# A GRU step's z seed moved behind the second half's new h, with one x unit between z and candidate

## The chip, the core and the metric

The kernel runs on one core of a Trainium2 chip. Its five engines work side by side, each through its own queue in order: TensorE (PE, with weight loads listed as PEld) multiplies matrices into PSUM, VectorE (DVE) and ScalarE (ACT) do element-wise work, GpSimd (POOL) does element-wise work on SBUF alone, and SyncE (SP) issues most of the transfers. The metric is the device time of one execution in microseconds, as a median over runs. Before the change it is 1341.13 us (three runs, 1340.63 to 1342.07).

## The reference

A gated recurrent unit over 128 time steps, with a batch of 64 rows and 512 features, whose outputs are added to the input. Every fourth step passes the state through one more layer.

```python
def step(h, inp):
    x_t, prop = inp
    comb = jnp.concatenate([x_t, h], axis=-1)
    z = jax.nn.sigmoid(comb @ Wz + bz)
    r = jax.nn.sigmoid(comb @ Wr + br)
    comb2 = jnp.concatenate([x_t, r * h], axis=-1)
    h_cand = jnp.tanh(comb2 @ Wh + bh)
    h_new = (1.0 - z) * h + z * h_cand
    h_next = jnp.where(prop, jnp.tanh(h_new @ Wp + bp), h_new)
    return (h_next, h_new)
```

`prop` holds where (t + 1) % 4 == 0, but for the last step. Everything is float32, the initial h is `cond_1024`, and the result is x plus the sequence of h_new.

## The kernel before

Each gate's matrix has an upper part that multiplies x_t and a lower part that multiplies h (or r * h). The lower products depend on the step before. The upper ones do not, and the kernel uses them to fill the time in which TensorE would wait.

**Two halves.** The batch is cut into two halves of 32 rows. The generator `half(h)` writes out the whole recurrence for one half, and a loop at the end takes the next piece from the half that is behind by a count of matmul columns, with the second half (h = 1) starting 700 columns later. The schedule is manual: the order in which instructions are written out is the order of each engine's queue. A matmul of one half uses 32 columns of the array, and each half has two such column groups of the four, so both halves can run at once.

**One step of a half.** On TensorE: gate R (four units), gate Z (four units), then `fill(places[0])` units of x, gate H for the candidate (four units, on rhT, the transposed r * h), then `fill(places[1])` units of x. In a step with `prop`, gate P follows (four units, on hT, the transposed new h) and then `fill(places[2])` units of x. A unit is two matmuls, each of which the trace shows as two records: 256 columns wide in the gates, 192 wide in the x units of the middle steps. Behind R come two sigmoids (`scratch_r`, L230), the product with h (`rh`, L807) and a transpose (`rhT`, L233). Behind Z of the second half come the four sigmoids for both halves at once, and `keep` = (z - 1) * h (L821). Behind H come two tanhs (`c`, L230), the product with z (L849, written over z in the PSUM bank), the subtraction of `keep` (`h`, L858) and the transpose (`hT`, L233). The next R, or P in a step with `prop`, needs that hT.

**Seeds.** The x part of a gate with its bias does not come through TensorE at the right time; it is prepared in an SBUF tile `cp`, and `seed(i, t, h)` (L371) has ScalarE copy it into the gate's PSUM place before the products with h are added onto it. R and H are seeded for each half (64 partitions), Z for both halves at once (128 partitions). The places: `rec_0` and `rec_1` hold R and H (or P) of one half each; `rec_z` is one bank that holds the sums of gate Z in its first half of the columns and z itself, later c, in the other. In a step with `prop` ScalarE also copies the bias of P (`bias_p`, L861) into `rec_0` and `rec_1`.

**Units of x.** The x products of eight steps are computed together, with fewer products than the plain way takes and more additions. They come as batches of 14 units in a fixed order of PSUM banks: two for bank a, two for x (where `scratch_x` and `scratch_y` take turns from batch to batch), two each for q and r, and then again two each for x, q and r. The second pair on x, and that on q, adds onto what the first left. When the second half has done the last unit of a pair, an `end` function is written out: for the first pair on x a copy of the bank to `cx` on ScalarE, for q a copy to `cq` (both L497), for r two additions on VectorE (L514, L515), and behind the second pairs another copy of q and three additions (L520, L523, L524). GpSimd joins the results of the batches into `cp` (L556, L561).

**Places.** `PLACES` gives the three numbers of x units for u = (t - 3) % 8, that is, for the steps 5 to 117; `HEAD` and `TAIL` give the first five and the last ten steps. Steps with u = 0 and u = 4 have `prop`. In the middle of the kernel the units of a group of eight steps add up to seven batches, so that each u always meets the same part of a batch: in step 67 (u = 0) a new batch begins.

The order on ScalarE in a step, where the seed of z stands: sigmoids of R, seed of R for each half, sigmoids of z, the seed of z for the next step, copies of `cx` or `cq` from x units behind Z, tanhs of the first half, seed of H or the bias of P, tanhs of the second half, again the seed of H or the bias of P, copies of `cx` or `cq`.

Of the kernel before, what the change touches and what calls it, by code (L numbers as in the profile page):

```python
# [18 lines left out]
def kernel(  # L19
# [28 lines left out]
    R, Z, H_ = range(3)  # L48
# [110 lines left out]
    def gate_ps(i, h):  # L159
        return rec[2][:, 0] if i == Z else rec[h][:, 0 if i == R else 1]  # L160
# [52 lines left out]
    def gate(i, h, lT, w):  # L213
        for k in range(K):
            products(gate_ps(i, h), h, lT[:, h, ts(k, V)], lambda c: quarters(w)[:, c, k])
            yield S * J
# [11 lines left out]
    def crossed(dst, h, i, func):  # L228
        for d in range(2):
            nc.scalar.activation(dst[ts(d, 2 * V)], gate_ps(i, h)[ts(h, 2 * V), d, :], func)  # L230

    def turn(dst, src):
        nc.vector.transpose(out=dst, in_=src)  # L233
# [44 lines left out]
    def sum_outer():  # L278
        for ka in range(S):
            nc.vector.tensor_sub(tw[3][:, ka], outer(1, 1, ka), outer(0, 1, ka))  # L280
            nc.vector.tensor_add(tw[2][:, ka], tw[3][:, ka], outer(0, 0, ka))
            nc.vector.tensor_sub(tw[4][:, ka], outer(1, 0, ka), tw[2][:, ka])
# [10 lines left out]
    def sum_inner_1(i, eng):  # L293
        eng.tensor_sub(inner(i, 0, 1), inner(i, 0, 1), inner(i, 0, 0))
# [17 lines left out]
    def sum_raw34(g):  # L312
        v = xT[g]
        sx[g, 34] = one.tile([P, 4, C, B], F32, tag="s73", name=f"s34r_{g}")
        four([sx[g, 34][:, n] for n in range(4)], v[:, 2], v[:, 3])
# [52 lines left out]
    def seed(i, t, h):  # L368
        if t < T:
            rows = slice(None) if i == Z else ts(h, 2 * V)  # L370
            nc.scalar.copy(  # L371
                gate_ps(i, h)[rows].rearrange("p d (c n) -> p d c n", c=C),
                G[t][rows, :, :, i, :].rearrange("p c d n -> p d c n"),
            )
# [224 lines left out]
    def pair_right(a, p1, x_, g=1):  # L599
# [2 lines left out]


    PLACES = (
        (0, 8, 6), (0, 8, 0), (6, 8, 0), (6, 8, 0), (0, 8, 6), (0, 8, 0), (6, 8, 0), (6, 6, 0),
    )
    HEAD = {0: (12, 12, 0), 1: (8, 6, 0), 2: (16, 12, 0), 3: (8, 6, 8), 4: (6, 8, 0)}
    TAIL = {
# [42 lines left out]
    def new_two(name, t):  # L651
        return shared(t, name, lambda: two.tile([P, S, J], F32, tag=name, name=f"{name}_{t}"))

    def new_turned(tag, name, t):
        return shared(t, name, lambda: new_T(tag, f"{name}_{t}"))

    def begin(t):
        u = (t - 3) % 8
        even = FIRST + 2 * ((t - 3) // 8)
        if t == 0:  # L660
            put(plain(2) + plain(3))
        elif t == 1:
            put(batch((1, 0), [(1, 1), (1, 2)]))
        elif t == 2:
            put(batch((1, 1), [(1, 10), (1, 11)]) + batch((1, 2), [(1, 8), (1, 9)]))
        elif t == 3:
            put(batches(FIRST))
        elif u == 7:
            put(batches(even + 2))
        if t == T - 10:  # L670
            put(
                batch((LAST, 0), [(LAST, 1), (LAST, 2)])
                + batch((LAST, 1), [(LAST, 10)])
                + plain_last()
            )

    def behind_r(t, duo, u):
        odd = FIRST + 2 * duo + 1
        if t == 1:
            for i in (5, 7):  # L680
                sum_inner(i, nc.gpsimd)
                sum_inner_1(i, nc.gpsimd)
        if t == 2:
            pair_left(0, 1, 2)
        elif t == 3:
            pair_right(0, 1, 10)
        if t == T - 7:
            pair_left(0, 1, 2, LAST)
        elif t == T - 6:
            pair_right(0, 1, 10, LAST)  # L690
        if t == 2:
            sum_inner(4, nc.gpsimd)
            sum_inner_1(4, nc.gpsimd)
        if u == 0 and duo >= 1 and odd - 2 < LAST:
            outer_u2(odd - 2)

    def join(t, duo, u, n):
        even, odd = FIRST + 2 * duo, FIRST + 2 * duo + 1
        if t == 0:
            join_x(0, 2 + n)  # L700
        elif t == 1:
            join_x(1, 2 + n)
        elif t == 2:
            join_x(2, n)
        elif t == 4:
            join_x(3, 2 * n)
            join_x(3, 2 * n + 1)
        elif duo >= 0 and u in (5, 6):
            join_x(even + 2, 2 * (u - 5) + n)
        elif duo >= 1 and u in (1, 3):  # L710
            join_x(odd, u - 1 + n)
# [78 lines left out]
    def half(h):  # L790

        for t in range(T):
            g, j = divmod(t, Q4)
            prop = j == CHUNK - 1 and t < T - 1
            last = t == T - 1
            duo, u = divmod(t - 3, 8)
            places = HEAD.get(t) or TAIL.get(t) or PLACES[u]
            if h == 0:
                begin(t)
            h_old, hT = state[t]  # L800

            yield from gate(R, h, hT, wh[R])
            if h == 1:
                behind_r(t, duo, u)
            rh, rhT = new_two("rh", t), new_turned("rhT", "rhT", t)
            crossed(r_, h, R, AF.Sigmoid)
            nc.vector.tensor_mul(rh[:, h, :], r_, h_old[:, h, :])  # L807
            turn(rhT[:, h, :], rh[:, h, :])
            if t != 3:
                seed(R, t + 1, h)  # L810
            if last:
                seed(H_, t, h)
            if h == 1:
                join(t, duo, u, 0)

            yield from gate(Z, h, hT, wh[Z])
            keep = new_two("keep", t)
            if h == 1:
                for i in range(S):
                    crossed(z[:, i, :], i, Z, AF.Sigmoid)  # L820
                nc.vector.scalar_tensor_tensor(  # L821
                    out=keep, in0=z, scalar=1.0, in1=h_old, op0=ALU.subtract, op1=ALU.mult
                )
                join(t, duo, u, 1)
                if t == 1:
                    sum_raw34(1)
                if t == 3:
                    for i in range(S):
                        seed(R, t + 1, i)
                seed(Z, t + 1, 0)  # L830
                if last:
                    nc.gpsimd.tensor_sub(xr[g][:, j], xr[g][:, j], keep)
                if t == 0:
                    sum_outer()
                    sum_inner(6, nc.gpsimd)
                    sum_inner_1(6, nc.gpsimd)
                if t == 2:
                    for n in range(2, 4):
                        join_x(2, n)
            yield from fill(places[0], h)  # L840
            if h == 1 and t == T - 7:
                reload()

            yield from gate(H_, h, rhT, wh[H_])
            h_new = new_two("h", t)
            cand = new_two("c", t)
            crossed(cand[:, h, :], h, H_, AF.Tanh)
            c = z[:, h, :]
            nc.vector.tensor_mul(c, cand[:, h, :], c)  # L849
            if last:  # L850
                o = xr[g][:, j, h, :]
                nc.vector.tensor_add(o, c, o)
                (nc.sync, nc.scalar)[h].dma_start(
                    out=out[ts(h, V), t, :].rearrange("b (q n) -> q b n", q=NQ), in_=o
                )
                return
            hT = new_turned("hT", "hT", t)
            nc.vector.tensor_sub(h_new[:, h, :], c, keep[:, h, :])  # L858
            turn(hT[:, h, :], h_new[:, h, :])
            if prop:  # L860
                nc.scalar.copy(gate_ps(P_, h)[ts(h, 2 * V)], bias_p[ts(h, 2 * V)])  # L861
            elif t < T - 2:
                seed(H_, t + 1, h)
            state[t + 1] = h_new, hT
            yield from fill(places[1], h)
            if h == 1 and t == 0:
                sum_outer_1()
                for i in (1, 2, 3):
                    sum_inner_1(i, nc.vector)
            if prop:  # L870
                yield from gate(P_, h, hT, wp)
                h_next = new_two("hprop", t)
                hT = new_turned("hT", "hpT", t)
                crossed(h_next[:, h, :], h, P_, AF.Tanh)
                turn(hT[:, h, :], h_next[:, h, :])
                if t < T - 2:
                    seed(H_, t + 1, h)
                state[t + 1] = h_next, hT
                yield from fill(places[2], h)
            if h == 1:  # L880
                behind_step(t, duo, u, h_new)
# [6 lines left out]
    while any(live):  # L888
        h = 0 if live[0] and (not live[1] or at[0] <= at[1]) else 1
# [45 lines left out]
```

## Time and profile before

| | |
|---|---|
| Median of three runs | 1341.13 us |
| The profiled execution, its own time | 1340.09 us |
| Span in the profile, first to last instruction | 1338.2 us |
| Mean granted TensorE clock | 0.992 |
| Chain that ended last: PE, ACT, DVE, DMA | 77%, 9%, 7%, 3% |
| Seed of z (`rec_z<-cp`, L371), 128 times | 0.377 us each |
| Tanh for 128 columns (`c`, L230), 512 times | 0.272 us each |
| Copies to `cx` and `cq` (L497) | 0.478 us each |

In the profile a group of instructions is named by line, engine, operation, and output<-input tile. Behind the bar stand its busy time, the mean of one in ns, and the idle time of the engine just before it with what ended it. In the timeline the columns are the start, the time, the engine, the line and the operation; "x2" are merged instructions, and the brackets hold idle time and what released it. The view of waits gives, for each waiting engine, line and releaser, the total, the number of times and the longest. The DMA engines are busy a tenth to a fifth of the time between the first tenth and the end of the span.

### The profile page before, as it was taken

The page shows a single profiled execution, that of the slowest core. Times are in us where ns is not written, and L with a number is a line of the kernel's source. Part 1 is how long each engine was busy: PE and PEld are TensorE (multiplying, and loading weights), DVE is VectorE, ACT ScalarE, POOL GpSimd, SP SyncE. Part 2 cuts the span into 40 slices and gives each one's busy share as a digit, 9 for nine tenths or more (in the row PEclk, how much of TensorE's full clock was granted, in tenths as well). Part 3 has the DMA queues.
Part 4 walks back from the last instruction along what each step waited for, and adds up shares of the span by engine and source line. Part 5 has one row for each costly group of instructions (what it writes and reads, how often), then busy time and mean ns, then how long its engine had stood idle before and what let it go on. Part 6 is the DMA issues. An engine that isn't in the chain of part 4 may idle for free.

```text
span 1338.2 us, 60949 instructions
## 1 busy us (share of the span) xinstructions
PE 1283.7 (96%) x26024; PEld 1117.0 (83%) x26024; DVE 771.2 (58%) x2163; ACT 837.1 (63%) x2688; POOL 886.3 (66%) x1030
## 2 busy tenths in 40 slices
PE   7989999999999999999999999999999999999977
PEld 3579888898988889888898988889888888988745
DVE  1645655656655656656556656656666566566534
ACT  1346666666666666666666666666666666666644
POOL 3568767677576776767777576777757777676410
PEclk8989999999999999999999999999999999999999
DMA  8401111101111111112101111111112111111040
GB/s 193 102 19 50 50 35 50 45 24 50 50 50 35 35 46 38 50 35 60 40 23 46 50 50 34 37 48 35 50 42 58 35 32 41 46 34 35 18 104 18
DMA packets 114710, 63.20 MB, mean 47 GB/s; under 512 B 13160, under 2 KB 109672, under 8 KB 114440
## 3 DMA queue, kind: packets, MB, share of 16 engines
q1 hardware_dynamic: 113412, 58.44, 17.3%
q8 instruction: 205, 3.36, 1.1%
q10 hardware_dynamic: 772, 0.72, 0.2%
q14 instruction: 65, 0.53, 0.1%
q0 software_dynamic: 256, 0.14, 0.1%
HBM read 42.47 MB, written 16.78 MB: 44 GB/s over the span
## 4 chain that ended last, share of the span: by engine, by line
PE 77%; ACT 9%; DVE 7%; DMA 3%; issue 2%; POOL 1%; SPq 1%; DVEq 0%; ACTq 0%; POOLq 0%
PE rec L204 35%; PE rec_z L204 15%; PE scratch_r L204 10%; PE scratch_q L204 9%; ACT rec_z L230 5%; PE scratch_x L204 3%; PE scratch_y L204 3%; PE scratch_a L204 3%; ACT c L230 2%; DVE keep L821 2%; ACT rec_z L371 2%; DVE hT L233 1%; DVE rec_z L849 1%; DVE h L858 1%; DMA wx<-in_L_cond_Wr_dram 1%
## 5 line engine op out<-in xcount | busy, mean ns | idle before, releaser
L204 PE MATMUL rec<-wh,rhT 128*32 128x256 f32 x4096 | 375.2, 381 | 4.6 <-ACT rec L371 4.4
L204 PE MATMUL rec<-wh,hT 128*32 128x256 f32 x3072 | 277.9, 380 | 14.7 <-DVE hT L233 14.7
L204 PE MATMUL rec_z<-wh,hT 128*32 128x256 f32 x3072 | 279.4, 379 | 0.0
L204 PEld LDWEIGHTS rec<-wh,rhT 128*32 128x32 f32 x4096 | 232.4, 110 | 35.6 <-ACT scratch_r L230 9.7
L230 ACT ACTIVATE scratch_r<-rec 64x128 f32<-64x128 f32 x512 | 128.0, 250 | 166.6 <-PE rec L204 95.6
L371 ACT COPY rec<-cp 64x256 f32<-64x256 f32 x512 | 189.9, 371 | 33.4 <-DVE cp L409 9.6
L204 PEld LDWEIGHTS rec<-wh,hT 128*32 128x32 f32 x3072 | 165.5, 110 | 48.0 <-ACT c L230 27.9
L230 ACT ACTIVATE rec_z<-rec_z 64x128 f32<-64x128 f32 x512 | 128.0, 250 | 108.1 <-PE rec_z L204 96.0
L204 PEld LDWEIGHTS rec_z<-wh,hT 128*32 128x32 f32 x3072 | 176.0, 110 | 14.4
L765 POOL TENSOR_TENSOR xr<-xr,h 128x256 f32<-128x256 f32 x127 | 93.0, 732 | 140.9 <-DVE h L858 122.8
L556 POOL TENSOR_TENSOR mb<-mb,mb 128x768 f32<-128x768 f32 x58 | 106.3, 1832 | 77.3 <-DVE mb L524 77.3
L230 ACT ACTIVATE c<-rec 64x128 f32<-64x128 f32 x512 | 139.0, 272 | 26.1 <-PE rec L204 16.8
L556 POOL TENSOR_TENSOR cp<-mb,mb 128x768 f32<-128x768 f32 x75 | 136.9, 1826 | 6.4 <-DVE mb L524 2.8
L556 POOL TENSOR_TENSOR cp<-mb 128x768 f32<-128x768 f32 x47 | 86.1, 1831 | 61.0 <-ACT rec L371 59.5
L821 DVE SCALAR_TENSOR_TENSOR keep<-rec_z,h 128x256 f32<-128x256 f32 x96 | 40.7, 424 | 144.9 <-ACT rec_z L230 144.9
L497 ACT COPY cq<-scratch_q 128x384 f32<-128x384 f32 (+1 forms) x214 | 102.0, 476 | 33.8 <-PE scratch_q L204 31.6
L204 PE MATMUL scratch_r<-wx,s12r 128*32 128x192 f32 x1056 | 120.9, 327 | 0.0
L204 PE MATMUL scratch_r<-tw,s 128*32 128x192 f32 x928 | 117.2, 326 | 0.0
L204 PE MATMUL scratch_r<-wx,s 128*32 128x192 f32 x928 | 107.3, 326 | 0.0
L514 DVE TENSOR_TENSOR cx<-scratch_r,cx 128x384 f32<-128x384 f32 (+1 forms) x107 | 59.2, 553 | 82.3 <-PE scratch_r L204 60.8
L849 DVE TENSOR_TENSOR rec_z<-c,rec_z 128x128 f32<-128x128 f32 x256 | 73.7, 288 | 54.8 <-ACT c L230 53.9
L204 PE MATMUL rec<-wp,hT 128*32 128x256 f32 x992 | 90.5, 380 | 12.1 <-DVE hT L233 12.1
(155 smaller groups left out, 3579.4 us busy)
## 6 DMA issues: line engine op xcount, KB each, us to landing
out_dram<-xr SPq DMA_DIRECT2D x249, 64.0 KB, 1.8
xr<-in_x_dram SPq DMA_DIRECT2D x248, 64.0 KB, 2.3
xs<-in_x_dram SPq DMA_DIRECT2D x240, 64.0 KB, 2.1
wx<-in_L_cond_Wz_dram SPq DMA_DIRECT2D x4, 256.0 KB, 8.2
wx<-in_L_cond_Wh_dram SPq DMA_DIRECT2D x4, 256.0 KB, 10.3
wh<-in_L_cond_Wr_dram SPq DMA_DIRECT2D x4, 256.0 KB, 9.0
wh<-in_L_cond_Wz_dram SPq DMA_DIRECT2D x4, 256.0 KB, 4.2
wh<-in_L_cond_Wh_dram SPq DMA_DIRECT2D x4, 256.0 KB, 7.4
```

The lines of the kernel that those rows point to most:

```text
L204: nc.tensor.matmul(ps[part(2 * h + c)], lhsT=left, rhs=rhs(c), start=start, stop=True, skip_group_check=True,)
L230: nc.scalar.activation(dst[ts(d, 2 * V)], gate_ps(i, h)[ts(h, 2 * V), d, :], func)
L233: nc.vector.transpose(out=dst, in_=src)
L371: nc.scalar.copy(gate_ps(i, h)[rows].rearrange("p d (c n) -> p d c n", c=C), G[t][rows, :, :, i, :].rearrange("p c d n -> p d c n"),)
L497: nc.scalar.copy(c[:, :nm], ps[:, :nm])
L514: nc.vector.tensor_add(T2[what][:, :nm], r_ps[:, :nm], T2[what][:, :nm])
L556: nc.gpsimd.tensor_add(dst, a, b)
L765: nc.gpsimd.tensor_add(xr[g][:, j], xr[g][:, j], h_new)
L821: nc.vector.scalar_tensor_tensor(out=keep, in0=z, scalar=1.0, in1=h_old, op0=ALU.subtract, op1=ALU.mult)
L849: nc.vector.tensor_mul(c, cand[:, h, :], c)
L858: nc.vector.tensor_sub(h_new[:, h, :], c, keep[:, h, :])
```

## The change

Two things. In `PLACES`, the steps with u = 0 and u = 4 take one x unit between Z and H in place of none, and one less behind P (5 in place of 6); those with u = 1 and u = 5 take one between Z and H and 7 in place of 8 behind H. The sums of the rows are what they were. And the seed of z for the next step is written out in another place: behind the second half's new h and its seeds, and so behind all tanhs of the step on ScalarE, where it stood in front of them. The lines between the two places have numbers one lower than before: L858 becomes L857, for instance.

```diff
     PLACES = (
-        (0, 8, 6), (0, 8, 0), (6, 8, 0), (6, 8, 0), (0, 8, 6), (0, 8, 0), (6, 8, 0), (6, 6, 0),
+        (1, 8, 5), (1, 7, 0), (6, 8, 0), (6, 8, 0), (1, 8, 5), (1, 7, 0), (6, 8, 0), (6, 6, 0),
     )
@@
                 if t == 3:
                     for i in range(S):
                         seed(R, t + 1, i)
-                seed(Z, t + 1, 0)
                 if last:
                     nc.gpsimd.tensor_sub(xr[g][:, j], xr[g][:, j], keep)
@@
             elif t < T - 2:
                 seed(H_, t + 1, h)
+            if h == 1:
+                seed(Z, t + 1, 0)
             state[t + 1] = h_new, hT
             yield from fill(places[1], h)
```

The instructions are the same in number and form on every engine; only their order changes, on TensorE and on ScalarE.

## The prediction

> **What bounds the kernel now.** I read the page first, then the list of waits, then the timeline of single steps. The page:
>
> ```profile
> span 1338.2 us, 60949 instructions
> PE 1283.7 (96%) x26024; PEld 1117.0 (83%) x26024; DVE 771.2 (58%) x2163; ACT 837.1 (63%) x2688; POOL 886.3 (66%) x1030
> L204 PE MATMUL rec<-wh,hT 128*32 128x256 f32 x3072 | 277.9, 380 | 14.7 <-DVE hT L233 14.7
> L204 PE MATMUL rec<-wp,hT 128*32 128x256 f32 x992 | 90.5, 380 | 12.1 <-DVE hT L233 12.1
> ```
>
> TensorE is the bound, and where it idles it waits for hT, the transposed new h. Idle time here understates the loss, because the modelled ends of earlier matmuls reach into the gap; I use distances between starts instead. The waits:
>
> ```profile
> PE rec L204 <- DVE hT L233: 26.7, 60, 1.6
> ACT rec_z L371 <- DVE keep L821: 61.8, 126, 0.5
> ```
>
> 60 waits for hT are about four in each group of eight steps, with u = (t - 3) mod 8 as the kernel counts them. The second line is the seed of z: it waits for `keep` 0.49 us in nearly every step, and ScalarE's queue waits with it. ScalarE in step 71 (u = 4):
>
> ```profile
> 769.17 1.09 ACT L230 ACTIVATE rec_z<-rec_z 64x128 f32<-64x128 f32 x4 [0.78 <-PE rec_z L204]
> 770.75 0.38 ACT L371 COPY rec_z<-cp 128x256 f32<-128x256 f32 x1 [0.49 <-DVE keep L821]
> 771.14 0.55 ACT L230 ACTIVATE c<-rec 64x128 f32<-64x128 f32 x2
> 771.72 0.37 ACT L861 COPY rec<-bias_p 64x256 f32<-64x256 f32 x1
> 772.12 0.56 ACT L230 ACTIVATE c<-rec 64x128 f32<-64x128 f32 x2
> ```
>
> The sigmoids of z end at 770.26, the tanh of the first half starts at 771.14: 0.88 us of seed lie between, though its matmuls had ended at 769.77. TensorE in the same step:
>
> ```profile
> 771.93 0.36 PE L204 MATMUL scratch_a<-wx,xT 128*32 128x192 f32 x2
> 772.10 0.36 PE L204 MATMUL scratch_a<-wx,xT 128*32 128x192 f32 x2
> 772.14 0.33 PE L204 MATMUL scratch_r<-tw,s4r 128*32 128x192 f32 x2
> 772.91 0.41 PE L204 MATMUL rec<-wp,hT 128*32 128x256 f32 x2 [0.44 <-DVE hT L233]
> 772.92 0.52 PE L204 MATMUL scratch_r<-wx,s12r 128*32 128x192 f32 x4
> 773.12 0.41 PE L204 MATMUL rec<-wp,hT 128*32 128x256 f32 x2
> ```
>
> Starts of one half are 0.21 us apart for 256 columns and 0.16 for 192, and a unit is two such: 0.43 us in a gate, 0.32 for x. The first half's P comes 0.81 after its last x, so 0.65 are lost; the second half's x stands still with it (772.14 to 772.92), so a waiting matmul holds all behind it.
>
> The same reading of the timeline for steps 67 to 74 (starts of R: 724.27, 736.48, 744.95, 754.72, 764.48, 776.58, 785.01, 794.84, 804.06) gives the losses of the first half by u. u0: 0.24 for rhT, 0.55 for hT. u1: 0.22 and 0.48. u4: 0.65. u5: 0.65. u2 and u3: 0.04 each. u6: 0.06. u7: 0.12 net, 0.15 of it for hT. Together 3.05 us in 79.8, and 14 such groups.
>
> **The change, step by step.** Times are from the start of R in the first half; the second runs 1.08 later (764.48, 765.56).
>
> u4. Z ends at 3.45, one x unit takes 0.32, H starts at 3.77, the eight x units at 5.50, P is due at 8.08. On ScalarE the sigmoids end as before at 5.78; H's last matmul ended at 5.29 and now at 5.61, so tanh starts at 5.80. From tanh to P it took 1.77 (771.14 to 772.91), so hT is there at 7.57, 0.51 early: minus 0.65.
>
> u5 and u1. Seven x units: R is due at 7.75. Here VectorE transposes x behind `keep` (782.74 to 783.17), which would end at about 6.6, after the tanh; the product then starts at 6.62, and from there to R it took 1.18 (783.83 to 785.01): 7.80. Some 0.05 stay: minus 0.60 in u5. In u1 the added unit also covers rhT's 0.22: minus 0.65.
>
> u2, u3, u6, u7. No units move, but the two scratch copies queued behind the seed start earlier, and so do their additions on VectorE. Between nothing and all of 0.08, 0.06 and 0.12; I take all, since in u6 the cx copy starts 0.03 after the seed ends (791.66, 791.69).
>
> u0. The added unit covers rhT's 0.24, or leaves up to 0.07, as the last scratch additions of u7 may come later; H starts at about 3.80, x at 5.53. But a new batch starts in u0. Its units in the changed order are a | a x x q q r r x | x q q r r around H and P, where they were nothing | a a x x q q r r | x x q q r r. The last x in front of P adds onto the bank that cx copies out. P, 1.72 us, used to lie between. That matmul waits for the copy, and the trace has this wait elsewhere, in u6 and u7, 0.29 each on weight loads:
>
> ```profile
> who waited for it (us, times):
> PEld scratch_y L204: 4.0, 14
> PEld scratch_x L204: 4.0, 14
> ```
>
> The x unit is due at 5.53 + 7 × 0.32 = 7.78. ScalarE's queue: tanh 5.80 to 6.37, bias copy to 6.77, tanh of the second half (its H ends at 6.72, 0.13 to the tanh) 6.85 to 7.41, bias copy to 7.81, then the moved seed. The seed waited for VectorE's last access to the bank of z, which was `keep`; now that is the second half's subtraction, 0.65 after its tanh (732.57 to 733.22): 8.06. Seed 8.09 to 8.47, cx 8.49 to 8.97, x unit at 9.03, as 0.06 lay between copy and matmul in u7. It stands 1.25, everything queued behind on TensorE with it: the second half's q, r and x units, then P. P starts at 9.35 instead of 8.54. The part behind P has one unit less (0.32), and the step ends 0.49 later than before. What is late next: cq's copy and its additions, needed after 11 us, so free.
> The ends for u0: minus 0.79 if that x unit never waits; plus 0.78 if the late cq copy costs a further wait of 0.29, the size of those for cx in the rows above. I take plus 0.49, from the queue.
> The Trainium skill (PSUM — Partial Sum Buffer, PSUM bank collisions raise a hardware error) asks to guard "by bank × quadrant (by bank is the simple version), not by address". The seed's wait for `keep`, which reads the bank's other columns, is that rule at work in 126 of 128 steps. Guarded by address the seed could start at 7.83, 0.26 earlier, and the total would be 1311; by the rule it is the sum below.
>
> Other queues. The seed is needed by Z of the next step, due at 7.75 + 1.72 = 9.47 at the earliest; it ends near 8.47, so 1.0 covers it (0.87 in u7). GpSimd writes into `cp` wait for the last seed (the `rec` copy held it 14 times for 4.3 us); the z seed is now last, 0.65 later, in front of 4 us of GpSimd idle time (749.63 to 753.70). No DMA moves.
>
> The last steps. In 123 to 126 the seed lies in front of tanh in the same way (1294.32 to 1295.20) and TensorE then waits for hT 1.0 to 2.2 us each: minus 0.86 four times, 3.4.
>
> Sum: minus 0.65 (u1), 0.65 (u4), 0.60 (u5), 0.08, 0.06, 0.12, plus 0.49 (u0) is minus 1.67, times 14 is 23.4, with the end 26.8. The profiled span of 1338.2 (1340.1 with what lies around it) becomes 1311.4. The median, 1341.1, stands 2.9 above the span; 1341.1 minus 26.8 is 1314.
>
> **Rivals.**
> A, no new wait in u0: the copy comes in time. Then u0 gains its 0.79 too, and the total is 14 × (2.16 + 0.79) + 3.4 = 44.7: 1296. For it: in u6 and u7 the copies are just in time. Against it: the queue above, which needs the second half's tanh and difference first.
> B, slower: the seed comes late for Z of the next step in the six steps without P. It must eat 26.8 / 14 = 1.91 per group, 0.32 in each, so it decides from about 1.2 to 1.3 us later than I put it. Were it queued behind cx and cq (0.96) and their wait for TensorE (0.5), it would be 0.5 past its slack and cost 6 × 0.5 × 14 = 42 on top of the forecast: 1356. Against it: in the changed order it stands in front of both copies.
> C, half the gain: something else on ScalarE or VectorE, such as the transpose of x, holds the product, so that u1, u4, u5 keep half their waits: 14 × 0.95 = 13 less, 1328. For it: u5 has no slack. Against it: u4 has 0.51.
>
> **How the numbers follow.** Forecast 0.70 (own range 1310 to 1322: u0 off by 0.29 either way is 4, and 0.15 more left in u1 and u5 would be another 4 upwards), A 0.17, C 0.06, no change within 0.2% (2.7 us, about what a measurement can tell from nothing) 0.02, B 0.05. The time is the forecast's, 1314; the range goes down to A, 1295, and up to 1322, and leaves out C, B and the ends of the others. Faster is forecast, A and C, 0.93; same 0.02; slower 0.05.
>
> **What would show it.** In u1, u4 and u5 tanh of the first half right behind the sigmoids of z, no wait for hT in front of P or R, R to R near 7.8, 11.45 and 7.8 us. In u0 R to R near 12.7, with about 1.2 us in front of an x unit, released by cx, and the z seed just ahead of cx. In the list of waits the seed waits for h (L857), not `keep`. It is wrong if u0 shows no wait for cx (A), if Z waits for its seed (B), or if hT still holds P in u4 (C).

## The result and the profile after

The changed kernel takes 1309.62 us (median of four runs, 1309.20 to 1313.06), against 1340.88 for the kernel before on the same chip. The ratio is 0.977, with a 95% interval from 0.975 to 0.979: some 31 us faster. 1314 was forecast, in a range from 1295 to 1322. The profiled execution has a span of 1307.3 us at a granted clock of 0.993 (1338.2 at 0.992 before).

The page of the changed kernel, the lines that answer to those shown of before:

```profile
span 1307.3 us, 60823 instructions
PE 1263.1 (97%) x26024; PEld 1085.0 (83%) x26024; DVE 774.2 (59%) x2163; ACT 837.9 (64%) x2688; POOL 887.4 (68%) x1030
L204 PE MATMUL rec<-wh,hT 128*32 128x256 f32 x3072 | 277.7, 379 | 2.1 <-DVE hT L233 2.1
```

TensorE's idle time in front of R, which needs hT, went from 14.7 to 2.1 us; in front of P it went from 12.1 to 0.8. The view of waits of the changed kernel (who waits, for whom, total, times, longest):

```profile
ACT rec_z L371 <- DVE h L857: 39.3, 127, 2.1
PEld scratch_x L204 <- ACT cx L497: 9.0, 7, 1.3
PEld scratch_y L204 <- ACT cx L497: 9.0, 7, 1.3
PE scratch_x L204 <- ACT cx L497: 6.4, 7, 0.9
PE scratch_y L204 <- ACT cx L497: 6.4, 7, 0.9
PE rec L204 <- DVE hT L233: 2.9, 4, 0.8
```

The seed of z now waits for the subtraction (L857) where it had waited for `keep`. Of the 60 waits for hT four are left, all of them from step 119 on. And there is a new wait: 14 times, once in each group of eight steps, an x unit waits for the copy to cx: its weight load stands idle 1.3 us, its matmul 0.9. ScalarE in step 71 (u = 4), in its timeline:

```profile
754.92 1.09 ACT L230 ACTIVATE rec_z<-rec_z 64x128 f32<-64x128 f32 x4 [0.77 <-PE rec_z L204]
756.04 0.55 ACT L230 ACTIVATE c<-rec 64x128 f32<-64x128 f32 x2
756.62 0.37 ACT L860 COPY rec<-bias_p 64x256 f32<-64x256 f32 x1
```

The tanh follows 0.03 us behind the last sigmoid; it was 0.88. TensorE in the same step, around the start of P:

```profile
758.21 0.33 PE L204 MATMUL scratch_y<-tt,s 128*32 128x192 f32 x2
758.22 0.33 PE L204 MATMUL scratch_r<-wx,s12r 128*32 128x192 f32 x2
758.37 0.39 PE L204 MATMUL rec<-wp,hT 128*32 128x256 f32 x2
758.38 0.49 PE L204 MATMUL scratch_a<-tw,o 128*32 128x192 f32 x4
```

From the first half's last x start to P are 0.16 us, the bare distance of two such matmuls, where there were 0.81. In step 67 (u = 0) the seed has become the obstacle in another place. ScalarE:

```profile
717.15 0.56 ACT L230 ACTIVATE c<-rec 64x128 f32<-64x128 f32 x2
717.74 0.37 ACT L860 COPY rec<-bias_p 64x256 f32<-64x256 f32 x1
718.39 0.38 ACT L371 COPY rec_z<-cp 128x256 f32<-128x256 f32 x1 [0.28 <-DVE h L857]
718.79 0.48 ACT L497 COPY cx<-scratch_y 128x384 f32<-128x384 f32 x1
719.92 0.48 ACT L497 COPY cq<-scratch_q 128x384 f32<-128x384 f32 x1 [0.65 <-PE scratch_q L204]
```

and TensorE:

```profile
718.00 0.36 PE L204 MATMUL scratch_r<-wx,s12r 128*32 128x192 f32 x2
718.05 0.36 PE L204 MATMUL scratch_q<-wx,xT 128*32 128x192 f32 x2
719.32 0.36 PE L204 MATMUL scratch_y<-tt,xT 128*32 128x192 f32 x2 [0.91 <-ACT cx L497]
719.34 0.36 PE L204 MATMUL scratch_q<-wx,xT 128*32 128x192 f32 x2
719.51 0.33 PE L204 MATMUL scratch_y<-tt,xT 128*32 128x192 f32 x2
719.52 0.33 PE L204 MATMUL scratch_q<-wx,xT 128*32 128x192 f32 x2
719.67 0.39 PE L204 MATMUL rec<-wp,hT 128*32 128x256 f32 x2
```

The copy to cx ends at 719.27 and the x unit on the same bank starts 0.05 later. The second half's q unit, which needs nothing of it, starts only then as well, since it stands behind. From start to start the wait costs 1.18 us: the first half's last r starts at 718.00, and P, due three starts of 0.16 later, comes at 719.67.

The distance from R to R of the first half, from the timeline, is the same to 0.01 us in nearly all groups, so that a table of eight numbers tells where the time went:

| u | 0 | 1 | 2 | 3 | 4 | 5 | 6 | 7 | sum |
|---|---|---|---|---|---|---|---|---|---|
| before, us | 12.21 | 8.47 | 9.77 | 9.77 | 12.10 | 8.43 | 9.84 | 9.22 | 79.8 |
| after, us | 12.75 | 7.78 | 9.73 | 9.73 | 11.46 | 7.78 | 9.73 | 9.08 | 78.0 |
| forecast of the difference | +0.49 | -0.65 | -0.04 | -0.04 | -0.65 | -0.60 | -0.06 | -0.12 | -1.67 |
| measured difference | +0.54 | -0.69 | -0.04 | -0.04 | -0.64 | -0.65 | -0.11 | -0.14 | -1.74 |

(The sums are of unrounded distances.) 14 groups make 24.4 us. From R of step 118 to the end it was 104.7 us and is 98.6, another 6.1. The two spans differ by 30.9.

### The profile page after: what moved, and what is told of

Same layout as the page of the kernel before. It is cut to its first block, busy times and chain, and to the rows that moved or that the text cites. A ratio compares the mean times of both kernels' runs of the same rounds, so it can differ in the third digit from the quotient of the medians.

```text
span 1307.3 us, 60823 instructions
## 1 busy us (share of the span) xinstructions
PE 1263.1 (97%) x26024; PEld 1085.0 (83%) x26024; DVE 774.2 (59%) x2163; ACT 837.9 (64%) x2688; POOL 887.4 (68%) x1030
## 4 chain that ended last, share of the span: by engine, by line
PE 88%; DMA 4%; DVE 2%; ACT 2%; SPq 2%; POOL 1%; issue 1%; DVEq 0%; POOLq 0%
PE rec L204 41%; PE rec_z L204 15%; PE scratch_r L204 13%; PE scratch_q L204 9%; PE scratch_a L204 4%; PE scratch_y L204 3%; PE scratch_x L204 3%; DMA xr<-in_x_dram 1%; DVE rec_z L848 1%; DVE h L857 1%; SPq L97 1%; ACT c L230 1%; DMA wx<-in_L_cond_Wz_dram 1%; DMA wh<-in_L_cond_Wr_dram 1%; ACT cx L497 1%
## 5 line engine op out<-in xcount | busy, mean ns | idle before, releaser
L204 PEld LDWEIGHTS rec<-wh,rhT 128*32 128x32 f32 x4096 | 226.8, 110 | 38.9 <-ACT rec L371 4.8
L204 PEld LDWEIGHTS rec_z<-wh,hT 128*32 128x32 f32 x3072 | 172.4, 110 | 8.2
L204 PE MATMUL scratch_q<-tt,s 128*32 128x192 f32 x928 | 100.0, 326 | 0.0
L561 POOL TENSOR_TENSOR mb<-mb,bias_x 128x768 f32<-128x768 f32 x35 | 64.2, 1835 | 51.8 <-DVE mb L524 51.8
```

Source lines behind the costliest of these rows:

```text
L204: nc.tensor.matmul(ps[part(2 * h + c)], lhsT=left, rhs=rhs(c), start=start, stop=True, skip_group_check=True,)
L561: nc.gpsimd.tensor_add(m, m, v.unsqueeze(1).to_broadcast([P, 2, 3 * J]))
```

## The experiments

Each kernel ran on one chip together with the kernel before; the ratios are to that, with their 95% intervals. The diffs of the first two are against the kernel before, the others against the changed one.

**The seed alone.** The table of places stays as it was.

```diff
-                seed(Z, t + 1, 0)
                 if last:
...
+            if h == 1:
+                seed(Z, t + 1, 0)
             state[t + 1] = h_new, hT
```

> The seed of z is moved, the table of places stays as it was. My theory: the seed in front of the tanhs made the waits for hT, the added x unit is not needed for them, and the wait of an x unit for cx in the steps with u = 0 comes from the added unit alone. Then R to R should be near 11.9 us for u = 0 (rhT is waited for by some 0.44, cx not at all), 8.0 for u = 1, 11.45 for u = 4, 7.8 for u = 5, and a group of eight 77.4 against 78.04 with the whole change: 14 times 0.61 less, 1301 us. Rival, the added unit makes the gain: near the time before, 1335 us or more.

1303.78 us, ratio 0.972 (0.970 to 0.973). R to R is 11.92 for u = 0, 8.00 for u = 1, 11.46 for u = 4, 7.78 for u = 5, and 77.42 for a group. As in the changed kernel, only four waits for hT are left, from step 119 on:

```profile
PE rec L204 <- DVE hT L233: 2.9, 4, 0.8
```

rhT is waited for by 0.46 in u = 0 and 0.22 in u = 1. The second part of the change is not needed for the gain, and as it stands costs more than it brings. The steps came as expected. The time is some 3 us above the expected 1301; in the profile R of step 7 starts 2.4 us later than in the changed kernel, and steps 122 and 123 take 1.6 us longer.

**The places alone.**

```diff
-        (0, 8, 6), (0, 8, 0), (6, 8, 0), (6, 8, 0), (0, 8, 6), (0, 8, 0), (6, 8, 0), (6, 6, 0),
+        (1, 8, 5), (1, 7, 0), (6, 8, 0), (6, 8, 0), (1, 8, 5), (1, 7, 0), (6, 8, 0), (6, 6, 0),
```

> The table of places is changed, the seed of z stays in front of the tanhs. My theory: hT still comes 8.43 us after R, so u = 5 and u = 1 keep R to R of about 8.43, u = 4 saves only the unit that left the place behind P (0.32), and u = 0 loses about 0.6, since an x unit in front of P waits for cx, which now is queued behind even later tanhs. Sum plus 0.26 for a group, 14 times: 1344 us, 0.3% slower than before. Rival, the added unit makes the gain: near 1310 us.

1342.66 us, ratio 1.001 (1.000 to 1.002): no gain, and at most a small loss. Its view of waits has both obstacles at once:

```profile
ACT rec_z L371 <- DVE keep L821: 62.0, 126, 0.5
PE rec L204 <- DVE hT L233: 17.9, 33, 1.7
PEld scratch_y L204 <- ACT cx L497: 14.9, 21, 1.5
PEld scratch_x L204 <- ACT cx L497: 14.7, 21, 1.5
```

R to R is 12.85 for u = 0 (0.64 more, an x unit waits 1.40 there), 8.34, 11.78 and 8.43 for u = 1, 4 and 5, and 80.01 for a group, 0.23 more than before where 0.26 were expected. Of the 60 waits for hT 33 are left: one in front of R behind each u = 1 and u = 5, and five in the last steps. In u = 4 hT comes no earlier: P starts 8.42 us after R, as before. The added unit fills half of the 0.65 that were lost there, and the 0.32 that the step gains are the unit that left the place behind P. In u = 0 the wait for cx has taken the place of that for hT. The rival, that the added unit makes the gain, falls.

**One unit back in u = 0.** The x unit between Z and H stays, but is taken from those in front of P, so that the unit which adds onto cx's bank stands behind P again.

```diff
-        (1, 8, 5), (1, 7, 0), (6, 8, 0), (6, 8, 0), (1, 8, 5), (1, 7, 0), (6, 8, 0), (6, 6, 0),
+        (1, 7, 6), (1, 7, 0), (6, 8, 0), (6, 8, 0), (1, 8, 5), (1, 7, 0), (6, 8, 0), (6, 6, 0),
```

> The whole change, but in the steps with u = 0 the places are (1, 7, 6): the unit for the place between Z and H is taken from those in front of P, so that the last x unit, which adds onto the bank that cx copies out, stands behind P again. My theory: the wait for cx, 1.17 us in each such step, goes and nothing takes its place, since hT is there 7.6 us after R and P is due at 7.9. R to R near 11.57 for u = 0, 14 times 1.18 less: 1293 us. Rival, that time is lost to hT or to something else on TensorE's queue in any case: no change, 1309 us, or half of it.

1295.73 us, ratio 0.966 (0.964 to 0.968). R to R for u = 0 is 11.60 where it was 12.75, a group takes 76.88, and no wait of a matmul for cx is left among the longest. So the wait was all that stood there: 14 × 1.15 are 16 us, and the medians differ by 14; in the profile steps 122 and 123 take 2 us of it back (23.4 where the changed kernel had 21.4). It is faster than both kernels. It also has 0.54 less in a group than the seed alone (77.42), 0.32 in u = 0 and 0.22 in u = 1: so much is the x unit between Z and H worth where it does not bring the wait for cx.

**The seed behind cx in steps with P.**

```diff
-            if h == 1:
+            if h == 1 and not prop:
                 seed(Z, t + 1, 0)
             state[t + 1] = h_new, hT
             yield from fill(places[1], h)
+            if h == 1 and prop:
+                seed(Z, t + 1, 0)
```

> The whole change, but in steps with the layer P the seed of z is written out behind the x units of the place in front of P, and so behind the copies to cx and cq. My theory: in the steps with u = 0 cx is late by what the seed takes and waits for (VectorE's subtraction in the bank of z), 0.64 us; the copy then follows the bias copy directly, and the wait falls from 1.17 to about 0.53. 14 times 0.64 less: 1300.6 us. Rival, the copy is held by the tanhs and the bias copies alone, and the seed in front of it costs nothing: 1309 us.

1302.17 us, ratio 0.971 (0.969 to 0.972). The wait falls from 1.18 to 0.52, R to R for u = 0 from 12.75 to 12.09. In ScalarE's timeline of step 67 the copy to cx follows the bias copy:

```profile
714.58 0.37 ACT L860 COPY rec<-bias_p 64x256 f32<-64x256 f32 x1
714.97 0.48 ACT L497 COPY cx<-scratch_y 128x384 f32<-128x384 f32 x1
716.10 0.48 ACT L497 COPY cq<-scratch_q 128x384 f32<-128x384 f32 x1 [0.65 <-PE scratch_q L204]
716.61 0.38 ACT L371 COPY rec_z<-cp 128x256 f32<-128x256 f32 x1
```

Of the 1.18 us 0.66 are thus the seed's and its own wait for the subtraction, and 0.52 come from the tanhs and bias copies, which stood in front of cx anyway, with the x unit moved in front of P.

**The old place in u = 0.**

```diff
-        (1, 8, 5), (1, 7, 0), (6, 8, 0), (6, 8, 0), (1, 8, 5), (1, 7, 0), (6, 8, 0), (6, 6, 0),
+        (0, 8, 6), (1, 7, 0), (6, 8, 0), (6, 8, 0), (1, 8, 5), (1, 7, 0), (6, 8, 0), (6, 6, 0),
```

> The whole change, but the steps with u = 0 keep their old places (0, 8, 6), while u = 1, 4 and 5 have the new ones. My theory: no wait for cx in u = 0, but rhT is waited for by 0.44 us there, without the x unit between Z and H. R to R near 11.9 for u = 0, 14 times 0.86 less: 1297.6 us. If the x unit between Z and H is worth nothing in u = 0, the same as with places (1, 7, 6), 1293 us.

1299.33 us, ratio 0.969 (0.968 to 0.971). R to R for u = 0 is 11.92, with 0.46 for rhT, against 11.60 with one unit back: the x unit between Z and H is worth 0.32 in this step, just its own length.

**The old seed in the last ten steps.**

```diff
-            if h == 1:
+            if h == 1 and t < T - 10:
                 seed(Z, t + 1, 0)
...
+                if t >= T - 10:
+                    seed(Z, t + 1, 0)
                 if last:
```

> The whole change, but in the last ten steps (118 to 127) the seed of z stands in front of the tanhs as before. The two traces differ by 6.15 us from step 118 to the end, where my sum had 3.4 for the steps 123 to 126. My theory: all of it is the seed's, since no place of these steps changed: 6.1 us slower than the whole change, near 1315.7 us. Rival, only the 3.4 are the seed's and the rest comes from the reload of the weights falling earlier: near 1313 us.

1314.59 us, ratio 0.981 (0.979 to 0.982), so 5.0 us above the median of the changed kernel. That lies between the two, but the intervals of the two ratios leave anything from 1.5 to 8 us, so the times alone do not decide. The timelines say more. From R of 118 to R of 122 it is 1.5 us more than in the changed kernel, from R of 124 to R of 127 it is 2.5 more, both just as in the kernel before, so both are the seed's. Steps 122 and 123 hold the wait for the reload of the weights: 23.7 us before and 21.4 after, but 21.6 here with the old seed, and between 22.9 and 23.4 in the six runs with the new seed in these steps and other places or another order before them. What decides that stretch is open; the two profiles of one and the same kernel, with one unit back, have 23.4 and 23.1. Behind the reload P of step 123 stands idle for hT by 1.64 us here and before, and by 0.79 in the changed kernel, so the seed costs 0.85 there as well, though the shorter wait for the weights hides most of it. Together the seed is worth 4.9 in the last steps, and the rest of the 6.1 between the profiles before and after lies in the wait for the weights. Neither expectation stands: not all of the 6.1 is the seed's, and more than the 3.4.

**The seed last.** One unit back in u = 0, and the seed behind all copies in all steps before the last ten; beside it the kernel with one unit back again. The diff is against the latter.

```diff
-            if h == 1:
+            if h == 1 and t >= T - 10:
                 seed(Z, t + 1, 0)
             state[t + 1] = h_new, hT
             yield from fill(places[1], h)
+            if h == 1 and t < T - 10:
+                seed(Z, t + 1, 0)
```

> Places (1, 7, 6) for u = 0 as in the run with one unit back, and in all steps before the last ten the seed of z behind the x units that follow H, so behind every copy to cx and cq of that place. It asks how late the seed may come. My theory: the copies and additions of u = 7 come 0.33 us earlier, so the 0.15 that H still waits for rhT in u = 0 go, 14 times 0.15: 2 us less, 1293.6 us; the seed ends some 0.25 to 0.3 before Z of the next step needs it. Rival, the one I had named as the way to a slower kernel: the seed is now too late for Z of the next step in the steps without P, up to 0.3 in six steps of a group, and the time rises by up to 25 us, to 1320.

> The same kernel as the run with one unit back, on the same chip as the one with the seed last, to compare the two: 1295.7 us.

1294.30 us with the seed last, ratio 0.963 (0.962 to 0.965), and 1295.03 for the other, 0.965 (0.963 to 0.966). The intervals overlap, so by the times alone the two are the same. In the traces R to R for u = 0 is 11.46 against 11.60 and the rest is equal, so 0.14 × 14, or 2.0 us, went as expected; the start of the kernel, which varies by some 3 us between the profiles, hides that in the times. No gate Z waits for its seed: in the six steps of a group without P it ends 0.16 us in front of the next Z (four of them) or 0.87 and 0.92, where it was 0.82 to 1.48 in the changed kernel. ScalarE at the end of step 66 with the seed last:

```profile
703.44 0.37 ACT L371 COPY rec<-cp 64x256 f32<-64x256 f32 x1
704.25 0.48 ACT L497 COPY cq<-scratch_q 128x384 f32<-128x384 f32 x1 [0.45 <-PE scratch_q L204]
704.76 0.38 ACT L371 COPY rec_z<-cp 128x256 f32<-128x256 f32 x1
```

The copy to cq waits for TensorE alone, and the seed ends at 705.14, with Z of step 67 starting at 705.30.

## Why the prediction was right, and where it was off

**hT was held by the seed, not by too little x work.** Right. Both parts were tried alone: the seed takes all waits for hT in the steps 5 to 117 away; the places alone leave those in front of R and only half fill the one in front of P in u = 4, and a group takes 0.23 longer than before.

**u4, u5 and u1.** Minus 0.64, 0.65 and 0.69, for 0.65, 0.60 and 0.65. The transpose of x on VectorE did not hold the product as I had put it: in step 68 the product starts at 729.51, 6.49 after R at 723.02, where I had 6.62 for it. The transpose runs there from 729.15 to 729.58 and the product starts before it ends, and the 0.05 that were to stay did not. Rival C, half the gain, falls with them.

**The wait for cx in u0.** Right in place, cause and size. From R, tanh came at 5.85 (5.80 by the prediction), the seed at 8.12 (8.09), cx at 8.52 (8.49), the x unit at 9.05 (9.03), P at 9.40 (9.35); plus 0.54 for 0.49. The 0.07 that might stay for rhT are 0.12. Rival A falls. What the prediction did not see is that the wait can go without giving up the unit: with (1, 7, 6) the unit stands between Z and H, and nothing waits for cx.

**The guard by bank.** The seed waited for the subtraction 127 times, although it writes columns of the bank that the subtraction does not read. That agrees with the rule of the Trainium skill (PSUM — Partial Sum Buffer, PSUM bank collisions raise a hardware error) to guard by bank and quadrant and not by address. In step 67 it is 0.28 us, from 718.11 to 718.39, and it goes on to cx; 0.26 had been put on it. No run gives z a bank of its own, so what the guard costs in the total is read from that wait and not tried.

**u2, u3, u6, u7.** Minus 0.04, 0.04, 0.11 and 0.14, the upper ends that were taken, and a little more.

**The slack of the seed.** Right for the changed kernel: no Z waits, with 0.82 to 1.48 us to spare where I had 1.0 and 0.87. Rival B falls. Its price for a seed behind cx and cq was too high: 0.5 past the slack in six steps, 1356 us. The run with the seed last puts it there, it still ends 0.16 us in front of Z in the tightest steps, and the time is 1294.30. I had added both copies and the wait for TensorE to one slack for every step. The step with the least to spare, 0.82, is delayed by 0.66 alone (in step 66, shown above, one copy and its wait stand in front of the seed), and where the delay is 1.32 there were 1.48 to spare.

**The last steps.** This is the term that was mis-sized: 3.4 us from four steps, 123 to 126, where the seed is worth 4.9. The waits of 118 to 121 were left out; they gave 1.5. The four steps that were counted gave what was said: 7.49 in place of 8.33 in 125 and in 126, 8.75 in place of 9.60 in 124, and in 123 P waits 0.85 less for hT.

Sum: 24.4 in the groups (23.4 by the prediction) and 4.9 at the end (3.4) make 29.3; the medians differ by 31.3 with an interval of some 2.5 either way (0.0019 of 1341). The groups came out 1.0 above the sum and the end 1.5 above it; the 2.0 that are left are within the interval.

## What to carry to other kernels

Look at what stands between the operands of a chain and its next instruction on an in-order engine: a copy that nobody needs soon, here 0.88 us with its own wait in front of the tanhs of every step, can cost more than its busy time tells. When it is moved, ask what stands behind it in its new place, and whether the second edit brings a consumer closer to exactly that: here one x unit moved across P turned a free copy into 1.2 us of standstill per group, and taking the unit from in front of P instead of from behind it kept the use of the unit without that wait (1295.7 us, against 1309.6, and 1303.8 for the seed alone). Two edits that come together are best tried apart; one of these was worth 2.8% and the other, alone, nothing; with its unit taken from the right place it added some 0.6% to the first.

## What the runs showed that I had not expected

The steady part repeats to 0.01 us in nearly every step, while two stretches that wait for transfers do not. R of step 7 starts between 125.0 and 128.4 us in the ten profiles, with the same units in front of it, and steps 122 and 123, with the reload of the weights, took 21.4 to 24.0. Each run has one profile, so how much of this is chance and how much the kernel's order is not shown; the one kernel with two profiles has 126.0 and 125.0, and 23.4 and 23.1. Differences below some 4 us between two medians are better read from the steps than from the totals.
